# Branching to the experts' widths before the first expert is prepared, with its first weights requested in the stage before

## The chip, the cores and the metric

The kernel runs on one NeuronCore of one Trainium2 chip. The metric is the device time of one execution in microseconds (us), as the median of repeated runs.

## The reference, cut to what matters

The program is one macaron block on 8 x 1024 tokens of 512 float32 values: half an expert layer, a self-attention layer, half an expert layer again, with a layer norm ahead of each.

```python
x = x + 0.5 * ffn(layernorm(x), w_router, w_gate, w_up, w_down)
x = x + attention(layernorm(x), Wq, bq, Wk, bk, Wv, bv, Wo, bo)
x = x + 0.5 * ffn(layernorm(x), w_router, w_gate, w_up, w_down)

def ffn(x, ...):                      # T = 8192 tokens, E = 32 experts, C = 320 rows for each
    probs = softmax(xt @ w_router)
    top1 = argmax(probs); gate = probs[top1]
    pos = (number of earlier tokens with the same top1)
    accepted = pos < C
    buf[top1, pos] = xt               # accepted tokens, by expert
    y = (silu(buf @ w_gate) * (buf @ w_up)) @ w_down
    return xt + where(accepted, y * gate, 0)
```

Every expert has three weight matrices of 512 x 512 (1 MB each). Which token goes to which expert, and how many each expert gets, is known only at run time.

## The kernel before, in words

The program has five parts in a row: the routing of all tokens (`front`), the experts (`experts`, first call), the attention (which routes its own results as it goes), and the experts again (second call). PE, ScalarE (ACT), VectorE (DVE) and GpSimd (POOL) run their instructions in the order in which the code writes them ("by hand"); SyncE (SP) issues the plain DMAs, in their order too.

**Routing.** Tokens are worked on in tiles of 128. `front` forms groups of tiles (4, then seven times 8, then 4). For each group `route` finds each token's expert, its place and its slot, and then GpSimd scatters a pair (token, gate) for every token into a table in HBM, with one indirect DMA for each tile (line 331). The tile `row` that these DMAs read has two buffers, so the row of one group waits for the scatters of the group two before it (lines 304 and 305). In the last group `sorted` ranks the experts by their number of tokens: it leaves a permutation `matrix`, the experts' `order` (line 466) and `arm`, the number of the narrowest of three width profiles that covers the counts (line 471).

**Experts, preparation.** `experts` has a preparation (lines 510 to 535) that holds for all profiles, then a `Switch` on `arm` into one of three copies of the loop over 32 experts. The preparation issues, on SP: the three weights of the first expert (line 578, by way of `load`), then the read of the whole table as `slots` (line 513, 96 KB). The table is reordered by two matmuls (line 519) into the row numbers `come` (to gather), `go` (to scatter) and the `gates`. GpSimd then gathers the rows of the first two experts, three blocks of up to 128 tokens each (line 587). The first expert is measured (`measure`: statistics of three blocks, line 151, then one power on GpSimd for all three, line 163), normalized on ACT (line 172), scaled for the residual on DVE (`rests`, line 186), and transposed (`transpose`: for each of four column parts k, three PE transposes and one copy on DVE, lines 658 and 661).

**Experts, loop.** `feed` computes one expert and prepares the next: measure the next, gather the one after that, then for each of four parts f the products with `w_gate` and `w_up` (line 670, accumulators `gp` and `up` with two buffers each), the gating on ACT and DVE (lines 675 and 694), at last the product with `w_down` (line 709) and an indirect DMA that scatters the results (line 727). The first call also moves tokens without a place (`all`, lines 600 to 615). The weights of the first expert lie in the preparation's pool, the others in a pool with two buffers inside the branch.

**Order on SP.** The first weights of the first call wait for the whole of `front`, its last scatter too: their memory is that of the routing's tiles. The attention begins with DMAs of the biases, the rotary tables and its weights.

Of the kernel before, what the change touches and what calls it, by code (L numbers as in the profile page):

```python
# [13 lines left out]
F32 = mybir.dt.float32  # L14
I32 = mybir.dt.int32
BF16 = mybir.dt.bfloat16
AF = mybir.ActivationFunctionType
ALU = mybir.AluOpType
AX = mybir.AxisListType
PSUM = bass.MemoryType.PSUM  # L20
DRAM = bass.MemoryType.DRAM

P = 128
# [5 lines left out]
G = 8  # L29
# [6 lines left out]
def at_once(steps):  # L36

    while True:
        try:
            next(steps)  # L40
        except StopIteration as end:
            return end.value
# [8 lines left out]
class Block:  # L51
# [287 lines left out]
    def front(self, pool, psum, x, rest, spare, carry, table, ranked):  # L339
# [2 lines left out]


        nc, NT, D, KD, E = self.nc, self.NT, self.D, self.KD, self.E
        sizes = [G // 2] + [G] * (NT // G - 1) + [G // 2]
        starts = [sum(sizes[:i]) for i in range(len(sizes))]
        group = [g for g, size in enumerate(sizes) for _ in range(size)]
        mv = pool.tile([P, NT, 2], F32, name="mv", bufs=1)
# [53 lines left out]
        for i in range(-ahead, NT + 2):  # L402
# [19 lines left out]
            t = i + ahead  # L422
# [49 lines left out]

        return (matrix, order, arm), rest()

    def experts(self, table, ranks, src, dst, w_gate, w_up, w_down, others=None):

        nc, tc, E, T = self.nc, self.tc, self.E, self.T
        NB, n = self.NB, self.last
        views = dram_disjoint_views(dst, E * NB + (self.NT if others else 0))
        weights = [w.rearrange("e (k p) f -> e p k f", p=P) for w in (w_gate, w_up, w_down)]
        F = mybir.EngineType
        by_hand = {F.PE, F.Activation, F.DVE, F.Pool}
        with tc.tile_pool(name="et", bufs=1) as tp:
            R = NB * E  # L490
            matrix, order, arm = ranks
            come, go = tp.tile([P, R], I32, name="come"), tp.tile([P, R], I32, name="go")
            at = [tp.tile([P, R], F32, name=f"at{i}") for i in range(2)]
            ids, gates = at

            def load(expert, r):
                e = nc.values_load(
                    order[0:1, r : r + 1], engines=[F.SP], min_val=0, max_val=E - 1,
                    skip_runtime_bounds_check_because="the number of a column of E",
                )  # L500
                return expert.load([w[e] for w in weights])

            acts = self.acts
            with (
                tc.tile_pool(name="ef", bufs=1) as fp,
                tc.tile_pool(name="efps", bufs=2, space=PSUM) as ps,
                tc.manual_schedule(engines=by_hand),
            ):

                expert = Expert(self, (tp, tp, ps), src, views, come, go, gates, acts)  # L510
                first = load(expert, 0)
                rows = fp.tile([R, P, 2], F32, name="slots")
                nc.sync.dma_start(
                    rows, table[0 : self.NS, :].rearrange("(r s) c -> r s c", s=P)
                )
                nc.vector.tensor_copy(rows[R - E : R, n:P, :], rows[R - E : R, 0:n, :])
                for i in range(2):
                    pt = ps.tile([P, R], F32, tag="tp", name="pt")
                    nc.tensor.matmul(pt, rows[:, :, i], matrix, start=True, stop=True)
                    if i == 0:  # L520
                        nc.vector.tensor_scalar(come, pt, float(T - 1), None, ALU.min)
                    nc.vector.tensor_copy(at[i], pt)
                states = [expert.gather(r, self.C) for r in range(2)]
                nc.vector.tensor_copy(go[:, 0 : R - E], ids[:, 0 : R - E])
                for i in range(2):
                    nc.vector.tensor_scalar(
                        go[i * n : (i + 1) * n, R - E : R], ids[i * n : (i + 1) * n, R - E : R],
                        2.0, float(i), ALU.mult, ALU.add,
                    )
                states[0].weights = first  # L530
                expert.measure(states[0])
                expert.scales(states[0])
                expert.normalize(states[0])
                expert.rests(states[0])
                expert.transpose(states[0])
            which = nc.values_load(
                arm[0:1, 0:1], min_val=0, max_val=len(self.profiles) - 1,
                skip_runtime_bounds_check_because="a sum of so many comparisons",
            )
            for i in tc.Switch(which, len(self.profiles)):  # L540
                with (
                    tc.tile_pool(name="ew", bufs=2) as wp,
                    tc.tile_pool(name="ea", bufs=2) as ap,
                    tc.tile_pool(name="eps", bufs=2, space=PSUM) as ps,
                    tc.manual_schedule(engines=by_hand),
                ):
                    expert = Expert(
                        self, (wp, ap, ps), src, views, come, go, gates, acts, others
                    )
                    now, following = (SimpleNamespace(**vars(state)) for state in states)  # L550
                    for r in range(E):
                        if following:
                            following.weights = load(expert, r + 1)
                        after = None
                        if r + 2 < E:
                            after = lambda: expert.gather(r + 2, self.profiles[i][r + 2])
                        now, following = following, expert.feed(now, following, after)


class Expert:  # L560


    def __init__(self, s, pools, src, views, come, go, gates, acts, others=None):
        self.s, self.nc, self.others = s, s.nc, others
        self.wp, self.ap, self.ps = pools
        self.src, self.views = src, views
        self.come, self.go, self.gates, self.acts = come, go, gates, acts

        self.xs = 3 if self.wp is not self.ap else 2

    def load(self, weights):
        nc, s = self.nc, self.s
        tiles = [
            self.wp.tile([P, k, d], F32, tag=name, name=name)
            for name, k, d in (("wg", s.KD, s.F), ("wu", s.KD, s.F), ("wd", s.KF, s.D))
        ]
        for t, w in zip(tiles, weights):
            nc.sync.dma_start(t, w)
        return tiles

    def gather(self, r, width):

        nc, s = self.nc, self.s
        NB = -(-width // P)
        x = self.ap.tile([P, s.NB, s.D], F32, tag="x", bufs=self.xs, name="x")
        for i in range(NB):
            nc.gpsimd.indirect_dma_start(
                out=x[:, i, :], out_offset=None, in_=self.src,
                in_offset=bass.IndirectOffsetOnAxis(
                    ap=self.come[:, i * s.E + r : i * s.E + r + 1], axis=0  # L590
                ),
            )
        return SimpleNamespace(r=r, width=width, NB=NB, x=x)
# [84 lines left out]
    def feed(self, now, following, after):  # L678
# [2 lines left out]

        nc, s = self.nc, self.s
        n, half, KF = s.last, s.D // 2, s.KF
        a, wd = self.acts[now.r % 2], now.weights[2]
        others = self.fetch_others(now.r) if self.others else None
        if following:
            self.measure(following)
# [663 lines left out]
def tile_macaron(  # L1351
# [22 lines left out]

    rest = [const.tile([P, NT], F32, name=f"rest{i}") for i in range(2)]
    spare = const.tile([P, NT], I32, name="spare")
    ranking = ctx.enter_context(tc.tile_pool(name="ranking", bufs=1))

    xf = x.rearrange("b l d -> (b l) d")
    of = out.rearrange("b l d -> (b l) d")  # L1380


    F_ = mybir.EngineType
    with (
        tc.tile_pool(name="a", bufs=2) as pool,
        tc.tile_pool(name="aps", bufs=4, space=PSUM) as psum,
        tc.manual_schedule(engines={F_.PE, F_.Activation, F_.DVE, F_.Pool}),
    ):
        none = pool.tile([P, s.NS // P, 2], F32, tag="none", bufs=1, name="none")
        nc.gpsimd.memset(none[:, :, 0], float(T))  # L1390
        nc.gpsimd.memset(none[:, :, 1], 0.0)
        for table in tables:
            nc.scalar.dma_start(
                table[0 : s.NS, :].rearrange("(p r) c -> p r c", p=P), none
            )
        ranks = []

        def ranked(counts):
            found, steps = s.sorted(ranking, psum, "lp", counts)
            ranks.extend(found)  # L1400
            return steps

        s.front(pool, psum, xf, rest, spare, zero, dram_disjoint_views(tables[0], NT), ranked)

    s.experts(tables[0], ranks, xf, x1, w_gate, w_up, w_down, (*rest, spare))


    attention = Attention(
# [2 lines left out]
    )  # L1411
    attention.run()

    s.experts(tables[1], attention.ranks, x2, of, w_gate, w_up, w_down)


def rope(L):
# [38 lines left out]
```

## Time and profile before

| what | us |
|---|---|
| median of 3 runs | 4938.32 (4932.55 to 4940.38) |
| the profiled execution: its time | 4953.15 |
| the profiled execution: its span, first to last instruction | 4951.4 |
| PE busy in the span | 4649.6 (94%) |
| DVE, ACT, POOL busy | 2842.6, 2923.9, 789.8 |

The mean granted TensorE clock is 0.969 of full speed. Times in the profile are microseconds from the start of the span. A row of the timeline gives the start, the busy time, the engine, the line of the kernel and what is written from what; in brackets stands the idle time before it, and what ended that. "PEld" is PE's weight load, "SPq" and "POOLq" are an engine's instruction queue. A DMA row gives the time to issue it; when its data has landed is seen from who waited for it. The chain of waits follows what ended last back to what released it.

### The profile page before, as it was taken

To read this page: it belongs to the slowest core of one execution; us is meant where nothing else is said; L and a number is where in the kernel's file an instruction comes from. 1 tells how busy PE (TensorE), PEld (TensorE's weight loads), DVE (VectorE), ACT (ScalarE), POOL (GpSimd) and SP (SyncE) were. 2 spreads that over 40 slices of the span, in tenths; PEclk is the share of its full clock that TensorE was granted. 3 is DMA by queue.
4 is the path that set the end of the run, shared out by engine and by line. 5 is a ranking of instruction groups with operands and counts; after the bars stand their busy time and mean duration, and the time that the engine had idled before them with its cause. 6 is when DMAs were issued, how large, how long until landed. Compare 5 with 4: busy or idle time off the path is not lost.

```text
span 4951.4 us, 68819 instructions
## 1 busy us (share of the span) xinstructions
PE 4649.6 (94%) x24568; PEld 2134.3 (43%) x24568; DVE 2842.6 (57%) x5530; ACT 2923.9 (59%) x5851; POOL 789.8 (16%) x779
## 2 busy tenths in 40 slices
PE   6499999969899999999999999999999876999998
PEld 4266667733233333333333333333333224666676
DVE  8333333337666777777777767767777633333332
ACT  6111112118999888888888888888888821111111
POOL 4323333210000010110110110100001002222221
PEclk8699999979999999999999999999999988999999
DMA  4355556630111212212212212212212124445553
GB/s 139 118 170 180 186 188 203 216 90 25 39 33 48 76 41 63 71 42 67 69 41 65 69 42 66 70 42 62 64 44 59 46 66 152 160 163 165 170 183 134
DMA packets 290535, 486.04 MB, mean 98 GB/s; under 512 B 47847, under 2 KB 83121, under 8 KB 290176
## 3 DMA queue, kind: packets, MB, share of 16 engines
q1 hardware_dynamic: 255328, 404.36, 26.0%
q0 software_dynamic: 34560, 76.93, 5.1%
q8 instruction: 197, 3.23, 0.3%
q14 instruction: 162, 1.33, 0.1%
q10 hardware_dynamic: 288, 0.20, 0.0%
HBM read 380.11 MB, written 89.72 MB: 95 GB/s over the span
## 4 chain that ended last, share of the span: by engine, by line
PE 81%; DVE 8%; ACT 4%; issue 3%; DMA 2%; POOL 1%; SPq 1%; another core or an unknown queue 0%; DVEq 0%; POOLq 0%; ACTq 0%
PE sa L1184 13%; PE gp L670 10%; PE up L670 9%; PE pq L1089 9%; PE po L1266 9%; PE yp L709 8%; PE sb L1164 5%; PE px L1292 4%; PE pv L1134 4%; PE sb L1191 3%; ACT junk L1203 2%; DVE nm L1199 2%; PE tp L658 2%; PE tp L194 2%; PE yp L717 1%
## 5 line engine op out<-in xcount | busy, mean ns | idle before, releaser
L1199 DVE TENSOR_REDUCE nm<-sa 128x2 f32<-128x1024 f32 x1024 | 1249.7, 1221 | 653.5 <-PE sa L1184 390.1
L1203 ACT ACTIVATE junk<-sa,nm 128x512 f32<-128x512 f32 x2048 | 1408.6, 688 | 256.1 <-DVE nm L1199 176.9
L1184 PE MATMUL sa<-k,q 32*128 32x512 f32 x4096 | 1150.4, 645 | 17.9 <-ACT junk L1203 11.5
L1196 ACT ACTIVATE pr<-sb 128x1024 f32<-128x1024 f32 x1024 | 1041.5, 1019 | 100.8 <-PE sb L1191 96.2
L1191 PE MATMUL sb<-q,k 32*128 32x512 f32 x4096 | 1062.8, 602 | 0.0
L675 ACT ACTIVATE sg<-gp 128x320 f32<-128x320 f32 (+3 forms) x256 | 103.0, 402 | 1228.7 <-PE gp L670 1091.7
L1266 PE MATMUL po<-pr,v 128*32 128x512 f32 x4096 | 549.5, 608 | 0.1
L1114 POOL TENSOR_TENSOR raw<-raw,a 128x512 f32<-128x512 f32 x128 | 165.0, 1289 | 2400.8 <-DMA rot<-raw 1638.9
L670 PE MATMUL gp<-bT,wg 128*128 128x320 f32 (+3 forms) x2048 | 532.6, 403 | 7.0 <-DVE n L167 6.2
L670 PE MATMUL up<-bT,wu 128*128 128x320 f32 (+3 forms) x2048 | 525.0, 399 | 0.0
L1089 PE MATMUL pq<-hT,wqk 128*128 128x512 f32 x1024 | 511.2, 623 | 4.7 <-DVE raw L1104 3.6
L709 PE MATMUL yp<-wd,a 128*128 128x512 f32 x1024 | 453.7, 596 | 0.0
L670 PEld LDWEIGHTS gp<-bT,wg 128*128 128x128 f32 x2048 | 387.6, 191 | 122.9 <-issue 35.6
L1164 PE MATMUL sb<-mrow,ones 3*128 3x512 bf16 x2048 | 393.8, 385 | 41.7 <-ACT pr L1196 40.0
L694 DVE TENSOR_TENSOR a<-sg,up 128x320 f32<-128x320 f32 (+3 forms) x256 | 114.1, 446 | 554.1 <-PE up L670 515.0
L670 PEld LDWEIGHTS up<-bT,wu 128*128 128x128 f32 x2048 | 389.2, 190 | 94.4 <-issue 0.2
L1164 PEld LDWEIGHTS <-ones 3*128 3x128 bf16 x2048 | 99.9, 91 | 710.8 <-issue 668.8
L1203 ACT ACTIVATION_READ_ACCUMULATOR junk<-sa,nm 128x1 f32 x2048 | 398.3, 195 | 0.0
L1191 PEld LDWEIGHTS sb<-q,k 32*128 32x128 f32 x4096 | 360.2, 184 | 0.1
L1184 PEld LDWEIGHTS sa<-k,q 32*128 32x128 f32 x4096 | 305.5, 184 | 80.7 <-ACT pr L1196 29.3
L1089 PEld LDWEIGHTS pq<-hT,wqk 128*128 128x128 f32 x1024 | 176.1, 191 | 323.5 <-issue 227.7
L713 DVE SCALAR_TENSOR_TENSOR ys<-yp,at,x 128x512 f32<-128x512 f32 x128 | 96.1, 751 | 369.0 <-PE yp L709 369.0
(171 smaller groups left out, 4275.0 us busy)
## 6 DMA issues: line engine op xcount, KB each, us to landing
wg<-in_w_gate SPq DMA_DIRECT2D x64, 1024.0 KB
wu<-in_w_up SPq DMA_DIRECT2D x64, 1024.0 KB
wd<-in_w_down SPq DMA_DIRECT2D x64, 1024.0 KB
rot<-raw SPq DMA_DIRECT2D x1024, 32.0 KB
xq<-in_x SPq DMA_DIRECT2D x16, 1024.0 KB
all<-in_x SPq DMA_DIRECT2D x32, 512.0 KB
xt<-first_rows SPq DMA_DIRECT2D x64, 256.0 KB
xr<-first_rows SPq DMA_DIRECT2D x64, 256.0 KB
```

The lines of the kernel that those rows point to most:

```text
L670: nc.tensor.matmul(acc, w[:, k, f * P : (f + 1) * P], to.bT[:, k, 0:width], start=(k == 0), stop=(k == s.KD - 1),)
L709: nc.tensor.matmul(yp, a[:, f, i * P : (i + 1) * P], wd[:, f, :], start=(f == 0), stop=(f == KF - 1),)
L1089: nc.tensor.matmul(acc, w[:, which, k, :], self.hT[b, n][:, k, :], start=(k == 0), stop=(k == KD - 1),)
L1134: nc.tensor.matmul(acc, hT[:, k, at : at + P], self.w_vo[:, k, :], start=(k == 0), stop=(k == KD - 1),)
L1164: nc.tensor.matmul(sb[:, h, :], self.ones16[at : at + 3, :], row[at : at + 3, :], start=True, stop=False,)
L1184: nc.tensor.matmul(sa[:, h, :], qa[at, (g * 4 + j) * P : (g * 4 + j + 1) * P], ka[at, m * 512 : (m + 1) * 512], start=True, stop=True,)
L1191: nc.tensor.matmul(sb[:, h, :], k[at, t * P : (t + 1) * P], q[at, n * 512 : (n + 1) * 512], start=False, stop=True,)
L1196: nc.scalar.activation(pr, sb, AF.Exp)
L1199: nc.vector.tensor_reduce(nm[:, m, j, pair : pair + 2], sa, AX.X, ALU.max, negate=True)
L1203: nc.scalar.activation(self.junk, sa[:, h - pair, :], AF.Exp, bias=nm[:, m, j, h : h + 1], accum_out=se[:, m, j, h : h + 1],)
L1266: nc.tensor.matmul(self.po[at : at + HD, :], self.v[b][t][:, c * P + at : c * P + at + HD], prs[h // 2 * 2][:, h % 2, :], start=(t == 0), ...
L1292: nc.tensor.matmul(acc, self.oT[b, c, half][:, j * P : (j + 1) * P], self.w_vo[:, c, :], start=False, stop=(c == KD - 1),)
```

## The change

There are four edits.

1. `front` splits the last group of 8 tiles into two of 4 (`sizes`).
2. After the routing, in its by-hand section, SP is given the loads of the weights of the first two experts of the first call, into a pool `et` with two buffers that is opened ahead of the routing's pools and closed after the experts. The second call of `experts` gets no loaded weights.
3. The `Switch` moves to the beginning of `experts`. Everything that was the preparation is now written in each of the three branches. In a branch the table is read first (`places`), then the first expert is gathered with the width of that profile; in the second call the weights of the first expert are requested after that.
4. The first expert is prepared by `begin`, block by block: statistics, power, normalization and four PE transposes for one block of tokens after the other, into four PSUM tiles at once; then the four copies, two on DVE and two on ACT; the scaling for the residual (`rests`) comes last, and the gather of the second expert after it in the code.

```diff
-        sizes = [G // 2] + [G] * (NT // G - 1) + [G // 2]
+        sizes = [G // 2] + [G] * (NT // G - 2) + [G // 2] * 3
...
+    def load(self, pool, order, r, weights):
+        nc = self.nc
+        e = nc.values_load(
+            order[0:1, r : r + 1], engines=[mybir.EngineType.SP], min_val=0,
...
+        for name, w in zip(("wg", "wu", "wd"), weights):
+            t = pool.tile([P, w.shape[1] // P, w.shape[2]], F32, tag=name, name=name)
+            nc.sync.dma_start(t, w.rearrange("e (k p) f -> e p k f", p=P)[e])
...
+    def experts(self, table, ranks, src, dst, weights, loaded=(), others=None):
...
+        which = nc.values_load(
+            arm[0:1, 0:1], min_val=0, max_val=len(self.profiles) - 1,
...
+        for i in tc.Switch(which, len(self.profiles)):
+            widths = self.profiles[i]
...
+                expert = Expert(self, (wp, ap, ps), src, views, others)
+                expert.places(table, matrix)
+                def load(r):
+                    return loaded[r] if r < len(loaded) else self.load(wp, order, r, weights)
+                now = expert.gather(0, widths[0])
+                now.weights = load(0)
+                expert.begin(now)
+                following = expert.gather(1, widths[1])
+                for r in range(E):
+                    if following:
+                        following.weights = load(r + 1)
...
+    def begin(self, to):
...
+        for i in range(to.NB):
+            at = slice(i, i + 1)
+            s.stats(ap, to.mv[:, i, :], to.x[:, i, :])
+            steps.append(s.normalizing(ap, to.mv[:, at, :], [t[:, at] for t in to.by]))
+            next(steps[i])
+            if i:
+                at_once(steps[i - 1])
+        at_once(steps[-1])
...
+        for i in range(to.NB):
+            s.normalize(to.b[:, i, :], to.x[:, i, :], to.by, i)
+            m = min(P, C - i * P)
+            for k, tp in enumerate(tps):
+                nc.tensor.transpose(
+                    tp[:, i * P : i * P + m], to.b[:m, i, k * P : (k + 1) * P],
+                    s.ident[:m, :m],
+                )
+        for k, tp in enumerate(tps):
+            (nc.scalar.copy if k % 2 else nc.vector.tensor_copy)(to.bT[:, k, 0:C], tp[:, 0:C])
+        self.rests(to)
...
+    first = ExitStack()
+    et = first.enter_context(tc.tile_pool(name="et", bufs=2))
...
         s.front(pool, psum, xf, rest, spare, zero, dram_disjoint_views(tables[0], NT), ranked)
+        loaded = [s.load(et, ranks[1], r, weights) for r in range(2)]
+    s.experts(tables[0], ranks, xf, x1, weights, loaded, (*rest, spare))
+    first.close()
...
-    s.experts(tables[1], attention.ranks, x2, of, w_gate, w_up, w_down)
+    s.experts(tables[1], attention.ranks, x2, of, weights)
```

`places` holds the lines of the old preparation that read the table and form `come`, `go` and `gates`, unchanged but for the pool of their tiles.

## The prediction

> **What bounds the kernel now.** I read the page first: busy shares, then the chain. Expert loops and attention are limited by PE, which nothing here changes: PE is busy 99.8 of 100 us in the stretch 309 to 409. The edits lie in the two places where PE idles: routing to first expert product (first call: PE's last routing product ends about 154, first `gp` at 209.41) and attention's end to the same product (`gp` at 4129.61). As each expert loop runs at PE's pace, an earlier first `gp` moves all that follows. So I ask for each call what ends last before `gp`. The chain of waits of the second call (start, length):
>
> ```profile
> 4094.49 2.13 DMA table<-row,slot
> ...
> 4098.86 9.90 DMA slots<-table
> ...
> 4113.83 7.13 DMA x<-x,come
> ...
> 4128.86 0.50 DVE bT L661
> ...
> 4129.61 4.61 PE gp L670 x8
> ```
>
> The reader sees serial work: last scatter, a table read of 9.90 us for 96 KB, the gather of token rows, and, in lines left out here, statistics, normalization and PE's ten transposes (3.12 us) up to the copy. Then the timeline of the first call:
>
> ```profile
> 169.06 0.96 POOL L331 DMA_INDIRECT table<-row,slot  x1 [0.31 <-issue]
> 171.73 0.39 SPq L578 DMA_DIRECT2D wg<-in_w_gate  x1
> 172.33 0.38 SPq L578 DMA_DIRECT2D wu<-in_w_up  x1
> 172.90 0.37 SPq L578 DMA_DIRECT2D wd<-in_w_down  x1
> 173.32 0.63 SPq L513 DMA_DIRECT2D slots<-table  x1
> 183.25 0.22 DVE L516 COPY slots<-slots 32x128 f32<-32x128 f32 x1 [24.52 <-DMA slots<-table]
> ...
> 193.27 0.69 DVE L151 BATCH_NORM_STATS2 st<-x 128x6 f32<-128x512 f32 x1 [7.55 <-DMA x<-in_x,come]
> ...
> 203.22 0.49 DVE L661 COPY bT<-tp 128x320 f32<-128x320 f32 x1 [0.42 <-PE tp L658]
> ...
> 209.41 3.88 PE L670 MATMUL gp<-bT,wg 128*128 128x320 f32 x8 [6.22 <-DVE n L167]
> ```
>
> The table read stands behind three weights in SP's queue. The last copy ends at 203.71, yet `gp` starts at 209.41; in the second call the same step takes 0.26 us (4129.35 to 4129.61). `gp` doesn't read `n`, so the releaser named is chance. Between copy and `gp` PE has only the Switch. The DMA answer for 204 to 209:
>
> ```profile
> DMA  9999999999999999999999999999999999999999
> ...
> q8 instruction: 1, 0.02, 1.4%
> ```
>
> The DMA engines are at nine tenths or more throughout, nearly all of it SP's queue (1.89 MB), and one block of code (0.02 MB, queue q8) comes in. I read the 5.4 us (5.70 less 0.26) as PE's fetch of the branch's code through busy DMA engines.
>
> **First call: Switch moved (edit 3).** All engines need `arm` only, ready at 157.28; PE, ACT and DVE then have nothing to do until the table lands at 183.25, so their jumps and fetches lie under that wait. Gain: PE's 5.4 us. [...] If the cover is gone, every engine that still waits for code pays about 5.4.
>
> **First call: weights early, table behind them (edit 2).** The weights no longer wait for the last scatter but for `order`. That looks like a gain of 15 us (156.42 to 171.73), but the table read stays behind them, and it is now 6 MB. Before, from the issue of `wg` to the table landed took 11.52 us with 3 MB; the queue moved some 395 GB/s, so 3.15 MB more are 8.0, in all 19.5. Also SP's queue holds under 4 MB (the third `wd` took 8.32 us to issue at 189.75, with 5.5 MB ahead): SP is held about 9 us in the issues before it reaches its own jump; within the 19.5.
>
> `order` itself comes later by edit 1. In the built order of DVE the chains of the last three groups of 4 are interleaved. Adding rows of the trace from 138.03 on: the four operations of the next group (0.32 each) and its ranking (1.7) now stand before the slots of tiles 44 to 51, so their scatters start at 144.5, not 141.34. The `row` of tiles 56 to 59 must wait until those 8 scatters (1.265 each) have landed: 155.5. Then follow 1.7 us of ranking, 0.8 for PE's count, 1.4 of sorting, 1.6 of slots, 1.2 of row: `order` at about 163, the last scatter ends at 171.6 (before 170.02). SP's first weight issues at 163.7 and the table lands at 163.7 + 19.5 = 183.2, against 183.25: **nothing gained**. Ends: `order` as before at 157 gives 177, 6 us better; scatters that land late under the weights (7.5 us, as a gather takes, not 2.13) end by 178, under the queue, at no cost; 3 us worse if SP's jump itself costs a fetch that leaves the queue empty.
>
> **Second call: table first.** SP's jump lies before the last scatter landed (4096.62). The table issues at 4097.2, as `wg` did, nothing ahead. How long alone? The nearest rows: a scatter 2.13 from its issue, and the program's first `xq` (1 MB, empty queue) 5.66, less 2.7 of data at 395 GB/s: 3.0. [...] A plain read from HBM is nearer to `xq`: with 3.0 it lands at 4100.2; before, DVE took it at 4108.88 (0.05 of it sequencer). Gain 8.6; ends 9.5 (2.13) and 5.7 (if POOL's own jump, begun at 4095.5, costs a fetch under load, ready 2 to 3 us after the row numbers). First weights now follow the table: 3 MB in by about 4108, long before `gp`; free.
>
> The gather after the table keeps its price: 2.47 from table to first gather, 7.5 to its first block, since weights fill the queues in both calls as before.
>
> **Preparation by blocks (edit 4).** Before, first block landed to `gp`: 4118.87 to 4129.61, 10.74. Now, from that landing (0), with the same rows: statistics with aggregate and the add 1.1 for a block; blocks land 1.1 apart. Power with its handovers 1.18, so block 0 has its factors at 2.4 (DVE is busy with block 1), ACT normalizes it 2.6 to 3.4; block 1 at 4.1, block 2 at 5.1 to 5.85 (0.8 each), four transposes of 64 columns to 6.5. Copies, 0.49 each, two on DVE beside two on ACT: first pair at 7.05. `gp` at 7.3. Gain **3.4** in each call: three serial things shrink, PE's 3.1 us of ten transposes, four copies in turn, and the residual scaling (2.1 us), which now runs on DVE under the first products. Powers go from one of 0.89 to three; POOL does them under DVE. Behind them in POOL's queue is the gather of the second expert: issued at 4.7 after landing, in by about 14 under load; DVE waits there for it with the first `a` behind it. PE has two `up` buffers and stalls only if `a` isn't done by 7.3 + 12.4 = 19.7; forecast 16.9. Free, with 2.8 us to spare.
>
> The `SiLU` table load (1.28 us, ACT) goes ahead of `gp`; ACT isn't late: 0. [...] its eight products may take the 4.61 of the second call, not 3.88: cost 0.7.
>
> **Attention's start.** In the built order of SP the three bias loads (issued 1024.11 to 1025.38) no longer wait for the last scatter of the experts, and `bo`, `wvo`, `xt` move up: gain 1.4, between 0 (if they queue elsewhere) and 1.5.
>
> **Sum.** First call 5.4 + 3.4 + 0.0 - 0.7 = 8.1. Second 8.6 + 3.4 = 12.0. Attention 1.4. Together 21.5 us: from the profiled span of 4951.4 to 4929.9. That execution took 4953.15, 14.8 above the median; the difference is taken from the median: 4938.3 - 21.5 = **4916.8**.
>
> **Rivals.**
>
> *The first call gains as well at the table* (chance 0.15): DVE's order costs less than I add up, `order` comes at 157. Then 6 us more: 4911. For: my sum adds rows that may overlap. Against: the wait of `row` for 8 scatters is in the program.
>
> *The first call gains nothing* (0.21): 6 MB ahead of the table, a late `order`, a late second gather (each us past 19.7 counts) or a PE jump that wasn't code take its 8.1: 4925, to 4929. For: the queue is shown full. Against: 5.4 us between copy and `gp` have no other owner.
>
> *It doesn't reach the end* (0.08): what is won is lost again where the loops or attention start: 4935. Against: PE is 99.8% busy there.
>
> *Slower: the jumps now lie on the path* (0.05). Place: after the Switch each engine of the chain table, `come`, gather, statistics, normalize, transpose starts on cold code while 6 MB of weights fill the DMA engines; fetches that come after an engine's data cost 5.4 each. With four exposed in all (of ten, five engines in two calls) the gain of 21.5 is gone; with seven: 7 x 5.4 = 38 less 21.5, so 4955. For: the PE stall at 203.71. Against: in the first call engines have 10 to 20 us between jump and data; in the second POOL has 7.
>
> *As summed*: 0.51, with 4911 to 4922 for the small terms.
>
> **Chances and range.** About 0.2%, 9.9 us, can be told from no change. Faster than 4928.4: as summed, the first rival, and nearly all of the second: 0.85. Same: the third and the second's edge: 0.10. Slower: 0.05. The range 4904 to 4929 takes in the first two rivals.
>
> **What would show it.** First call: PE, DVE, ACT and POOL jump before the table lands; no gap between the last copy and `gp`; table at about 183, in spite of weights issued at 164; `gp` near 201. Second call: table read issued before `wg`, landed 3 us later, `gp` near 4117 on the old clock, 12 us less from the last scatter to `gp`. In both, 7.3 us from first block to `gp`. It would be wrong if engines show idle time of "issue" for some 5 us inside the branches before the first `gp`, or if `order` is ready well before 163.

## The result, and the profile after

The changed kernel takes 4914.68 us (median of 5; 4911.93 to 4919.01), the kernel before on the same chip 4934.31 (median of 5): a ratio of 0.9958, with a 95% interval of 0.9943 to 0.9972, so 19.6 us less. The forecast was 4916.8, which is 21.5 less than the 4938.32 on record then (median of 3). On a second chip, where both kernels took longer, the ratio was 0.9951 (0.9937 to 0.9964; 4929.19 against 4954.69, 25.5 us less). As the absolute times differ by chip, everything below is compared by its ratio to the kernel before on the same chip, or by distances inside one trace.

The profiled execution of the changed kernel took 4919.01 us, with a span of 4917.2; PE is busy 4646.1 of it (94%), as before. Where the time went is read from the two stages in which PE idles. The timeline of the changed kernel in the first call (start, busy time, engine, line; in brackets the idle time before it):

```profile
147.50 0.39 SPq L485 DMA_DIRECT2D wg<-in_w_gate  x1
...
153.79 3.51 SPq L485 DMA_DIRECT2D wd<-in_w_down  x1
154.57 0.97 POOL L331 DMA_INDIRECT table<-row,slot  x1 [0.30 <-issue]
162.65 0.35 SPq L553 DMA_DIRECT2D slots<-table  x1
...
171.54 0.22 DVE L554 COPY slots<-slots 32x128 f32<-32x128 f32 x1 [22.29 <-DMA slots<-table]
...
180.33 0.69 DVE L151 BATCH_NORM_STATS2 st<-x 128x6 f32<-128x512 f32 x1 [6.19 <-DMA x<-in_x,come]
...
187.18 4.63 PE L692 MATMUL gp<-bT,wg 128*128 128x320 f32 x8 [0.26 <-DVE bT L600]
```

The weights are requested at 147.50, before the last scatter (154.57), and yet the table is taken only at 171.54. Between the end of the last scatter on GpSimd (155.54) and the issue of the table read stand 7.1 us, in which SyncE waits until the last scatter has landed (its semaphores come in from 158.5 to 162.6); then 8.9 us until the table is taken. PE's idle time in front of `gp` is 0.26 us, where it was 6.22. The stretches of the same trace between these events (start:end, length, busy time and count of PE, PEld, DVE, ACT, POOL, granted clock, DMA share, GB/s):

```profile
147.50:155.50 8.00, 0.00 (x0) 0.00 (x0) 1.55 (x10) 0.00 (x0) 6.16 (x7) 0.50 0.86 259
155.50:162.60 7.10, 0.00 (x0) 0.00 (x0) 0.00 (x0) 0.00 (x0) 0.04 (x1) 0.50 1.01 284
162.60:171.50 8.90, 0.00 (x0) 0.00 (x0) 0.00 (x0) 0.00 (x0) 0.00 (x0) 0.50 1.05 377
```

For 16 us no compute engine has anything to do: the core waits for weights that nobody needs yet, because a table of 96 KB is behind them. In the first two stretches, with scatters under way, the DMA engines moved 259 and 284 GB/s, in the third, without them, 377. Part of the first figure is the start of the first transfer (the engines' busy share is 0.86 there); in the second the engines are fully busy and still move a quarter less. The second call, in which the table goes first:

```profile
4077.49 0.34 SPq L553 DMA_DIRECT2D slots<-table  x1
4078.37 0.41 SPq L485 DMA_DIRECT2D wg<-in_w_gate  x1
...
4079.53 0.22 DVE L554 COPY slots<-slots 32x128 f32<-32x128 f32 x1 [9.17 <-DMA slots<-table]
...
4082.05 0.98 POOL L609 DMA_INDIRECT x<-x,come  x1 [6.58 <-DVE go L564]
...
4088.08 0.69 DVE L151 BATCH_NORM_STATS2 st<-x 128x6 f32<-128x512 f32 x1 [5.96 <-DMA x<-x,come]
...
4094.90 1.43 PE L692 MATMUL gp<-bT,wg 128*128 128x320 f32 x2 [0.26 <-DVE bT L600]
```

The same read takes 2.04 us here. It is 15.4 us from the table to `gp`, against 20.7 in the kernel before (4108.88 to 4129.61).

All profiles on one sheet. "Scatter to gp" runs from the end of the last scatter on GpSimd to the first product; "table" from the issue of its read until VectorE takes it; "block to gp" from the first gathered block measured. All in us, first call / second call. These distances don't contain the routing, and are the better measure of the edits: most of the versions' intervals overlap, so that their times alone can't rank them.

| kernel | ratio to before, 95% | scatter to gp | table | block to gp |
|---|---|---|---|---|
| before, profile shown above | 1 | 39.4 / 34.2 | 9.9 / 10.0 | 16.1 / 10.7 |
| before_again | timed once | 39.7 / 34.6 | 10.2 / 10.2 | 16.2 / 10.8 |
| changed kernel | 0.9958 (0.9943 to 0.9972) | 31.6 / 19.4 | 8.9 / 2.0 | 6.9 / 6.8 |
| after_again | 0.9951 (0.9937 to 0.9964) | 31.5 / 20.3 | 10.2 / 2.0 | 6.9 / 7.2 |
| switch_fixed | 1.0003 (0.9994 to 1.0011) | 36.6 / 36.2 | 10.0 / 9.8 | 13.2 / 12.7 |
| old_prep | 0.9968 (0.9957 to 0.9980) | 34.8 / 23.4 | 8.7 / 2.0 | 10.7 / 10.1 |
| table_line | 0.9956 (0.9943 to 0.9970) | 29.2 / 24.0 | 2.0 / 2.0 | 16.7 / 11.3 |
| no_split | 0.9946 (0.9932 to 0.9959) | 27.5 / 20.0 | 6.0 / 2.0 | 6.9 / 6.4 |
| table_act | 0.9949 (0.9936 to 0.9963) | 28.3 / 20.0 | 6.0 / 2.1 | 6.9 / 6.5 |
| one_early | 0.9934 (0.9921 to 0.9948) | 23.2 / 19.9 | 2.2 / 2.1 | 6.7 / 6.4 |
| table_first | 0.9927 (0.9913 to 0.9940) | 20.3 / 19.5 | 2.1 / 2.1 | 6.9 / 6.9 |
| quiet_gather | 0.9923 (0.9909 to 0.9936) | 17.8 / 17.0 | 2.0 / 2.1 | 6.4 / 6.9 |
| quiet_no_split | 0.9921 (0.9907 to 0.9934) | 17.9 / 17.0 | 2.1 / 2.0 | 6.4 / 7.0 |

### The profile page after: what moved, and what is told of

Its sections match the earlier page's. It is cut to its first block, busy times and chain, and to the rows that moved or that the text cites. A ratio compares the mean times of both kernels' runs of the same rounds, so it can differ in the third digit from the quotient of the medians.

```text
span 4917.2 us, 68877 instructions
## 1 busy us (share of the span) xinstructions
PE 4646.1 (94%) x24572; PEld 2133.2 (43%) x24572; DVE 2847.5 (58%) x5568; ACT 2925.1 (59%) x5856; POOL 789.9 (16%) x784
## 4 chain that ended last, share of the span: by engine, by line
PE 81%; DVE 8%; ACT 4%; issue 3%; DMA 2%; POOL 1%; SPq 1%; DVEq 0%; POOLq 0%; ACTq 0%
PE sa L1206 13%; PE gp L692 10%; PE up L692 9%; PE pq L1111 9%; PE po L1288 9%; PE yp L731 9%; PE sb L1186 5%; PE pv L1156 4%; PE px L1314 4%; PE sb L1213 3%; ACT junk L1225 2%; DVE nm L1221 2%; PE tp L680 2%; PE tp L194 1%; PE yp L739 1%
## 5 line engine op out<-in xcount | busy, mean ns | idle before, releaser
L1206 PE MATMUL sa<-k,q 32*128 32x512 f32 x4096 | 1150.0, 645 | 19.4 <-ACT junk L1225 12.0
L735 DVE SCALAR_TENSOR_TENSOR ys<-yp,gates,x 128x512 f32<-128x512 f32 x128 | 96.1, 751 | 369.0 <-PE yp L731 369.0
```

Source lines behind the costliest of these rows:

```text
L1206: nc.tensor.matmul(sa[:, h, :], qa[at, (g * 4 + j) * P : (g * 4 + j + 1) * P], ka[at, m * 512 : (m + 1) * 512], start=True, stop=True,)
```

## The experiments

**Theory:** in both calls the table read is what ends last; the gain comes from what shortens the way through it, and in the first call the early weights take back part of it. **Rivals:** the weights had to come early, the Switch is the main part, or the difference is of the routing (the profiled execution before was 34 us longer than the one after, of which 19.6 are the medians').

**before_again** and **after_again**: both kernels unchanged, for second profiles.

> The kernel before, unchanged, for a second profile. Theory: the idle time of 13.43 us of GpSimd ahead of the scatter at 141.34 belongs to that one execution (it took 14.8 us more than the median), so it is not here: last scatter at about 156.6, table at 169.9, first gp at about 196, span about 4937. The idle time of 5.4 us of PE between the last copy and gp is of the program and is here again. Rival 1: the idle time ahead of the scatter is here again, gp at 209. Rival 2: the 5.4 us are not here, and were part of the same disturbance.

> The changed kernel, unchanged, for a second profile and a second measurement. In four of the six profiles so far ScalarE stood idle for 13.4 to 13.7 us in all in the routing (before copies at 115 to 131, with nothing in the trace that released it), in one 7.2, in the profiled execution of the changed kernel not at all. Theory: this idle time is of the execution, not of the change, so it can be here too, and the last scatter is then issued at about 169 to 170; from the last scatter's end to the first gp it takes 31.6 us as in the first profile, against 39.4 in both profiles of the kernel before. Rival: it is of the change (another order of the routing's work avoids it), and the last scatter is at about 155 again.

The first expectation fell (its rival 1, that the idle time is there again, holds), and the second came true. The kernel before, again; what ScalarE waited for between 110 and 135 (us in total, times, longest):

```profile
ACT lg L240 <- remote: 6.5, 1, 6.5
ACT xT L408 <- remote: 5.3, 1, 5.3
ACT parts L230 <- remote: 1.6, 1, 1.6
```

The changed kernel, again; its timeline of ScalarE:

```profile
114.04 0.59 ACT L408 COPY xT<-tp 128x512 f32<-128x512 f32 x1
120.72 0.27 ACT L240 COPY lg<-lp 128x128 f32<-128x128 f32 x1 [6.10 <-remote]
120.89 0.81 ACT L172 ACTIVATE h<-xq,nmr,rstd 128x512 f32<-128x512 f32 x1
125.00 0.58 ACT L408 COPY xT<-tp 128x512 f32<-128x512 f32 x1 [3.29 <-remote]
129.99 0.58 ACT L230 COPY parts<-pl 128x512 f32<-128x512 f32 x1 [4.41 <-remote]
```

ScalarE stands idle for 13.4 and 13.8 us at the same three copies, with no releaser in the trace, in both kernels. Such idle time of 12.2 to 13.8 us in all (in table_first 7.2) is in the first profile of the kernel before (whose 4953.15 us are a time of the slower chips) and in all eight of the two chips on which that kernel takes 4951 and 4955 us. It is not in the first profile of the changed kernel, nor in the four of the chip on which the kernel before takes 4935. So in these 14 profiles it goes with the chip and not with the change, and comparing the first two profiles span by span would have credited the change with some 14 us that are not its own. The distances behind the routing repeat: 39.4 and 39.7 before, 31.6 and 31.5 after.

**table_first**: the early weights taken away.

```
-        loaded = [s.load(et, ranks[1], r, weights) for r in range(2)]
-    s.experts(tables[0], ranks, xf, x1, weights, loaded, (*rest, spare))
+    s.experts(tables[0], ranks, xf, x1, weights, (), (*rest, spare))
```

> The changed kernel, but the first call requests its weights as the second does: inside the branch, behind the table read; nothing is requested in the routing's section. Theory (the early weights hold up the table): in the changed kernel the last scatter landed some 7 us after its issue and the table was taken at 171.54, 8.9 us after the issue of its read. Without the 6 MB ahead the last scatter (issued 155.5) lands in about 2, the table 2.04 after that as in the second call: taken at about 159.7. From there the second call needs 15.4 to its first gp (4079.53 to 4094.90): gp at about 175 instead of 187.18, the time about 12 us less than the changed kernel, 4902 to 4904. Rival (early weights are needed at gp): the 3 MB, requested only at about 162, share the queues with the gather and the second expert's 3 MB, and gp waits for them: gp between 184 and 190, time 4912 to 4918.

Its timeline in the first call:

```profile
167.12 0.97 POOL L331 DMA_INDIRECT table<-row,slot  x1 [0.30 <-issue]
169.81 0.35 SPq L553 DMA_DIRECT2D slots<-table  x1
170.70 0.41 SPq L485 DMA_DIRECT2D wg<-in_w_gate  x1
...
171.89 0.22 DVE L554 COPY slots<-slots 32x128 f32<-32x128 f32 x1 [10.08 <-DMA slots<-table]
...
188.36 4.63 PE L692 MATMUL gp<-bT,wg 128*128 128x320 f32 x8 [0.27 <-DVE bT L600]
```

From the last scatter's end (168.09) to the table's issue 1.7 us, to the table 2.1, to `gp` 20.3 in all: 11.3 less than in the changed kernel, where 12 were expected. PE's idle time in front of `gp` is 0.27, so no weight is late. The whole takes 37.5 us less than the kernel before, against 19.6 and 25.5 for the changed kernel. (Its 4913.94 lies among the times that were expected of the rival, but these were formed on the first chip; on this one the kernel before takes 4951.39.) The early weights cost about a third of what the rest of the change gains: by the ratios 0.0024 to 0.0031 of 0.0073, by the distances 11.3 of 33.8 us.

**one_early** and **table_act**: only 3 MB early (`range(1)`, one buffer); and all 6 MB early with the table read on ScalarE's queue.

```
-        nc.sync.dma_start(rows, table[0 : s.NS, :].rearrange("(r s) c -> r s c", s=P))
+        (nc.scalar if self.others else nc.sync).dma_start(rows, table[0 : s.NS, :].rearrange("(r s) c -> r s c", s=P))
```

> The changed kernel, but only the first expert's weights (3 MB, not 6) are requested in the routing's section. Theory: these 3 MB, issued from 147.5, are in by about 158.5, when the last scatter (issued 155.5) can land by 159 to 160; the table follows by 162 and gp by 177 to 178: some 9 us less than the changed kernel, 4905 to 4907. Rival (it is not the bytes ahead that hold up the table): table at 171 as before, time within 2 us of the changed kernel's 4914.7.

> The changed kernel with the 6 MB early, but in the first call the table read is issued on ScalarE's queue instead of SyncE's. If the table is held up by its place in SyncE's queue, it now lands 2 to 5 us after its issue at about 162.7 (between 165 and 168, instead of 171.54), and the time falls by 4 to 7 us, to 4908 to 4911; the late landing of the last scatter (7 us) remains. If the DMA engines themselves serve the bytes in the order in which they were requested, whatever the queue, it lands at 171 again and the time is 4914 to 4916.

The last scatter, the issue of the table read and the copy that takes it; first one_early, then table_act (ACTq is ScalarE's queue):

```profile
170.49 0.97 POOL L331 DMA_INDIRECT table<-row,slot  x1 [0.30 <-issue]
...
176.25 0.36 SPq L553 DMA_DIRECT2D slots<-table  x1
...
178.42 0.22 DVE L554 COPY slots<-slots 32x128 f32<-32x128 f32 x1 [13.25 <-DMA slots<-table]
```

```profile
170.25 0.97 POOL L331 DMA_INDIRECT table<-row,slot  x1 [0.30 <-issue]
...
177.89 0.40 ACTq L553 DMA_DIRECT2D slots<-table  x1
...
183.84 0.22 DVE L554 COPY slots<-slots 32x128 f32<-32x128 f32 x1 [18.90 <-DMA slots<-table]
```

With 3 MB the last scatter still lands late (4.8 us from its end to the table's issue), but the table then has nothing ahead of it and takes 2.2: scatter to `gp` 23.2, 8.4 less than the changed kernel (9 expected). On its own queue the table takes 6.0 us, neither 2 nor the 8.9 and 10.2 of the changed kernel: some of the delay is the place in SyncE's queue, and some goes with the weights still under way (some 2.3 MB at its issue, an estimate: 6.3 MB less what the DMA engines would have moved in 14.7 us at the changed kernel's 259 and 284 GB/s). The last scatter, on a queue of its own too, landed 6.7 us after its end, where it was 7.1 and 5.6 in the changed kernel. Scatter to `gp` is only 3.3 shorter, and the ratio moves by 0.0002 to 0.0009, within the intervals; 4 to 7 us were expected. The hold-up has to be removed at the bytes, not only at the queue.

**table_line**: the kernel before with one line moved, `first = load(expert, 0)` behind the table's `dma_start`.

> The kernel before with one line moved: the read of the table is issued ahead of the first expert's weights, in both calls. Theory (the table's place in SyncE's queue is the largest part of the change): it is taken 2 us after its issue instead of 9.9 to 10.2 in both calls, so gp comes 8 to 9 us earlier in each, 16 to 18 us less than the kernel before. Rival (the weights or the gather take the place of the table): the 3 MB of weights are then late for the gather or for gp, and no more than 8 us are gained in all.

Its timeline in the first call:

```profile
171.73 0.35 SPq L512 DMA_DIRECT2D slots<-table  x1
...
173.76 0.22 DVE L516 COPY slots<-slots 32x128 f32<-32x128 f32 x1 [14.92 <-DMA slots<-table]
...
193.17 0.49 DVE L661 COPY bT<-tp 128x320 f32<-128x320 f32 x1 [0.42 <-PE tp L658]
...
199.29 3.88 PE L670 MATMUL gp<-bT,wg 128*128 128x320 f32 x8 [6.16 <-DVE n L167]
```

Scatter to `gp` falls by 10.2 in each call, more than forecast, because the gather comes in after 6.4 us instead of 7.5 as well. In time 22.8 us less, where the whole change gives 25.5 on the same chip; the intervals overlap. PE's gap in front of `gp` (193.66, the last copy's end, to 199.29) is still there, so it has nothing to do with the table.

**switch_alone** and **switch_fixed**: the kernel before with only the Switch moved ahead of the preparation. Of the edit, as switch_fixed has it, the lines that matter:

```
-        with tc.tile_pool(name="et", bufs=1) as tp:
+        for arm_i in tc.Switch(which, len(self.profiles)):
+            with tc.tile_pool(name="et", bufs=1) as tp:
...
-                            after = lambda: expert.gather(r + 2, self.profiles[i][r + 2])
+                            after = lambda: expert.gather(r + 2, self.profiles[arm_i][r + 2])
```

> The kernel before with one edit only: the Switch ahead of the preparation, which is otherwise as before (first weights first, then the table; statistics, normalization and transposes in the old order). Theory (PE's idle time ahead of the first gp is the fetch of the branch's code): 0.3 us between the last copy and gp instead of 5.7, so from the last scatter's end to gp 34 us instead of 39.4; no change in the second call, where the gap was 0.26. About 5 us less than the kernel before. [...] Rival 2 (the fetch comes at another place): engines show idle time of some 5 us inside the branch before gp, and the time is as before or slower.

> The Switch moved alone, as in the run switch_alone, with its fault mended: there an inner loop wrote over the number of the profile, so that every branch took the middle profile's wider products and both loops of experts were longer (some 30 us each). What that run showed up to the first gp stands: 0.58 us between the last copy and gp instead of 5.7, code blocks fetched at 155 to 162 instead of at 205, and 35.7 us from the last scatter's end to gp instead of 39.4; in the second call 35.7 instead of 34.2. Expected with the loops as before: first call 3 to 4 us less, second 1 to 2 us more, in all 1 to 3 us less than the kernel before. Rival (the second call's loss was of the fault too): 4 to 5 us less.

The first of them (ratio 1.0120, 1.0104 to 1.0135) had an inner loop that wrote over the number of the profile, so that all branches computed with the middle profile's widths; its loops are some 30 us longer each, and it says something only up to the first `gp`. The second is as meant, and gains nothing (1.0003), where 1 to 3 us were expected. Its timeline in the first call:

```profile
183.04 0.69 DVE L151 BATCH_NORM_STATS2 st<-x 128x6 f32<-128x512 f32 x1 [0.56 <-DMA x<-in_x,come]
...
187.72 1.90 PE L659 MATMUL tp<-ident,b 128*128 128x128 f32 x6 [1.67 <-DVE bT L662]
...
189.66 0.49 DVE L662 COPY bT<-tp 128x320 f32<-128x320 f32 x1 [0.42 <-PE tp L659]
190.21 0.50 PEld L671 LDWEIGHTS gp<-bT,wg 128*128 128x128 f32 x2 [0.77 <-DVE bT L662]
190.21 1.43 PE L671 MATMUL gp<-bT,wg 128*128 128x320 f32 x2 [0.58 <-DVE bT L662]
```

PE's idle time in front of `gp`, 6.22 us in the kernel before, is 0.58 here (from the last copy's end, 190.15, it is 0.06 instead of 5.70): that step is right. But once preparation and loop stand in one branch, their order on VectorE mixes: the statistics of the second expert's blocks (the one at 183.04 is the third of them) go ahead of the first expert's copies, and PE's transposes wait for those (1.67). Block to `gp` is 13.2 and 12.7 rather than the 10.7 expected without a gap: from scatter to `gp` 2.8 are gained in the first call and 2.0 lost in the second. In the changed kernel the second gather, and so its statistics, stand behind `begin`, and this doesn't occur.

**old_prep**: the changed kernel without `begin`; in its place `measure`, `scales`, `normalize`, `rests`, `transpose`.

> The changed kernel with edit 4 undone: inside the branch the first expert is prepared in the old order (all statistics, one power, all normalizations, residual scaling, then for each column part its transposes and one copy on VectorE), nothing else changed. Theory: from the first block to gp about 10.7 us instead of 6.85 in both calls, 7 to 8 us more than the changed kernel in all. Rival (the copies and transposes hide behind the arrival of the weights or the fetch of code): under 3 us more.

Its first call, from the first block to the last copy:

```profile
178.48 0.69 DVE L151 BATCH_NORM_STATS2 st<-x 128x6 f32<-128x512 f32 x1 [6.27 <-DMA x<-in_x,come]
...
189.15 4.63 PE L696 MATMUL gp<-bT,wg 128*128 128x320 f32 x8
189.26 0.49 DVE L687 COPY bT<-tp 128x320 f32<-128x320 f32 x1 [0.42 <-PE tp L684]
```

Block to `gp` is 10.7 and 10.1 us instead of 6.9 and 6.8 to 7.2: `begin` is worth 3.7 to 3.8 and 2.9 to 3.3. The ratio of 0.9968 is 0.0010 to 0.0017 above the changed kernel's, 5 to 8 us; its interval overlaps the changed kernel's two. Its 10.7 in the first call, against 16.1 in the kernel before with the same order of work, is also the cleanest measure of the Switch: 5.5 us. The lines show something that the prediction didn't have: with preparation and loop in one branch, `gp` starts before the last of the four copies does (189.15 against 189.26). In the second call, where the kernel before has no long gap, the moved Switch still brings 10.1 instead of 10.7.

**no_split**, **quiet_gather**, **quiet_no_split**: the last groups of tiles 8 and 4 as before; the version of table_first with all weights but the first `wg` held back; and both together. The holding back is a write of one element that the DMA has to follow, on VectorE after the statistics of the first block (for the first expert's `wu` and `wd`) or of the last (for the second expert's weights):

```
+        for j in which:
+            if hold:
+                nc.vector.memset(tiles[j][0:1, 0, 0:1], 0.0)
```

> The changed kernel with edit 1 undone: the last groups of tiles 8 and 4 as before. Theory (the split makes order late and so the early weights): order is ready about 5 us earlier (156.5 against 161.0 where ScalarE stood idle for some 13.5 us), the 6 MB start earlier and most of them are through when the last scatter is in; the table is taken at 178 to 180 instead of 185.7 in the second profile of the changed kernel, and the time is 5 to 7 us less than the changed kernel's. Rival (the last scatter is what counts, and the split brings it no later or even earlier): within 2 us of the changed kernel.

> The version with the table first in both calls and no early weights, and with the other weights held back: only the first expert's wg (1 MB) is requested behind the table; its wu and wd are requested when the first gathered block has been measured, the second expert's weights when the last block has been. (A one-element memset on VectorE holds each DMA back.) Theory (the gather's 6.0 to 7.0 us from issue to first block are time behind 3 to 6 MB of weights): the first block lands 3 to 4 us after its issue, gp comes 3 us earlier in each call, and the time is about 6 us less than with the table first alone. Rival 1 (the gather takes that long by itself): no difference at the block, the same time. Rival 2 (wu is now late): PE waits for wu after the first four products of gp, and the gain is lost again.

> The version with the table first in both calls and the other weights held back (quiet_gather), with edit 1 undone as well. Nothing is requested in the routing here, so only the last scatter's time counts. With the split and with about 13.5 us of idle ScalarE it was issued at 168.9 to 170.5, without the split at 168.1 to 169.3. Expected: gp 0 to 1.5 us earlier, the same time as quiet_gather within 2 us. Rival (the split does bring the last scatter earlier, as the two profiles of other idle times would allow): 1 to 2 us slower.

Without the split `order` is ready at 139.31 where it was 146.79 in the changed kernel's first profile (both without the idle time of ScalarE before these copies), the table takes 6.0 us, with some 5.1 of the 6.3 MB through at its issue (an estimate, again at 259 and 284 GB/s), and scatter to `gp` is 4.1 shorter; the ratio moves by 0.0005 to 0.0012, 2 to 6 us, within the intervals. With nothing requested early no difference of the split can be told (0.9921 and 0.9923). What it costs shows only in the distance, by way of the early weights.

Holding back the weights shortens the gather. In quiet_gather, second call:

```profile
4081.91 0.98 POOL L638 DMA_INDIRECT x<-x,come  x1 [6.66 <-DVE go L592]
...
4085.33 0.70 DVE L151 BATCH_NORM_STATS2 st<-x 128x6 f32<-128x512 f32 x1 [3.35 <-DMA x<-x,come]
```

The first block is there 3.4 us after its gather, instead of 6.1 in table_first; in the first call 5.1 instead of 7.0, as SyncE put the read of the tokens without a place (1 MB) ahead of it. Scatter to `gp` is 2.5 shorter in each call. That 5 us show in the time is not settled: the ratio is 0.0004 (2 us) below table_first's, within the intervals, where 6 us were expected. quiet_no_split has the lowest ratio of all, 0.9921 (0.9907 to 0.9934), 4895.37 against 4935.01 of the kernel before: 39.6 us less. By the ratios that is 1.6 to 1.9 times the change's gain.

## Why the prediction was right, step by step

The way of the change and most of its terms came out as forecast. That the sum came within 2 us is in part luck: from the last scatter to `gp` the first call gained 7.8 to 8.1, where the terms make 10.4 (5.4 + 3.4 and, with the last scatter 1.6 later and the table as before, 1.6), and the second 14.3 to 14.7, where they make 12.0. On a clock like that of the profile from which the forecast was made (after_again, with the same idle time of ScalarE) `order` came at 161.0 (forecast 163), the table at 185.68 (183.2) and `gp` at 201.45 (near 201). By the distances of the sheet:

- **Switch moved, 5.4:** right, and shown twice (old_prep's 10.7 against 16.1; in switch_fixed 0.06 us from the last copy to `gp` instead of 5.70). That it is a fetch of code fits: in the gap of the kernel before, a block of code (0.02 MB, queue q8) comes in between 206.4 and 207.0, and in that of table_line between 196 and 198 (before_again has one somewhere between 160 and 210); in the second call of the kernel before, without the gap, it comes at 4132, behind the start of the first `gp`; and in switch_alone it came in between 155 and 160, ahead of the table, and none from 160 to 205. But the trace doesn't say for which engine a block is, so the cause is inferred from this timing, and why the second call could do without the block stays open. That a moved Switch alone would keep the 5.4 was not claimed and isn't so.
- **Table behind 6 MB, "nothing gained":** the mechanism was right, a size wrong. The term "the queue moved some 395 GB/s, in all 19.5" measured 24.0 (147.50 to 171.54): until the last scatter had landed the DMA engines moved 259 and 284 GB/s, and the table read, issued only then, still had some 2.2 MB of weights ahead of it (an estimate: 6.3 MB less what these rates make in 15.1 us). Against the end of the last scatter the table came at 16.0 us, before at 13.2: a loss of 2.8, where the sum had a gain of 1.6 (11.6 us, 171.6 to 183.2). "At no cost" for the scatters that land late was wrong too: with nothing requested early the table is issued 1.7 us after the last scatter's end instead of 7.1, and from there to `gp` it is 11.3 us less (table_first).
- **`order` later by the split:** forecast 6.7 us later (163 against 156.33; the terms listed from 155.5 on add up to 162.2). The wait of `row` for the scatters is there: 4.75 us of idle VectorE up to 140.00 in the changed kernel's first profile. Versions with and without the split on chips of the same kind differ by 4.4 to 7.5. Last scatter: forecast 1.6 later, measured between 0.4 earlier and 2.6 later.
- **Table first in the second call, 8.6:** read 3.0 forecast, 2.04 measured. The value chosen, from `xq`, was too high; the lower bound (2.13, a scatter) was nearer. From the last scatter's end to the table it is 4.0 to 4.1 now and was 13.4 to 13.9: a gain of 9.4 to 9.9.
- **The gather keeps its 7.5:** wrong, in the changed kernel's two profiles it takes 6.0 to 6.6: 1.0 to 1.6 more gained in each call. quiet_gather shows that the number depends on what is queued ahead (5.1 in its first call, 3.4 in its second).
- **`begin`, 3.4 in each call:** forecast 7.3 from block to `gp`, measured 6.8 to 7.2. Against old_prep 3.7 to 3.8 and 2.9 to 3.3; in the second call some 0.7 more comes with the moved Switch, as `gp` starts before the last copy.
- **Clock, -0.7:** an estimate from the two calls of the profile before, where the first eight products took 3.88 (at a granted clock of 0.61) and 4.61 (at 0.50). In the first call of the changed kernel they took 4.63 (at 0.50) in one profile and 3.76 in the other: it varies without the change, and what sets it was not shown.
- **Second gather's margin:** in both calls of the first profile PE is busy 34.94 of the 35 us from the first `gp` on, at a granted clock of 0.93 and 0.92; in after_again it has no idle time in the 35 us of the first call, nor in the first 24 of the second: right.
- **Attention's start, 1.4:** the loads behind the biases are issued 2.99 us after the last result scatter, 4.40 before, as forecast. The first product with `wqk` then comes 42.8 us after the end of that scatter instead of 43.5 (in the second profiles 43.0 instead of 43.7): 0.7 to 0.8 is left. From the first `gp` of the first call to the last scatter of the attention it is 3888.3 and 3884.6 in the changed kernel's two profiles, 3886.0 and 3884.4 before: nothing that can be told.

In sum the two calls gain 22.1 to 22.8 between last scatter and `gp` (22.4 by the terms), less up to 2.6 where the split brings the last scatter later (forecast 1.6): between 19.5 and 23, beside the 19.6 and 25.5 of the medians (the interval of the second is 17.8 to 31.2). The rival in which exposed code fetches make it slower did not happen: in both profiles no engine has an idle time of over 1.1 us on "issue" inside the branch before `gp` but PE's weight load, whose 12.4 and 27.6 us lie under the wait for the table. The rival "the first call gains at the table" was nearest to what could have been had, but the lever was to request the weights later, not to have `order` earlier.

## What to carry to other kernels

A small transfer on which everything waits has to go ahead of the big ones that only need to be there later, and "ahead" means fewer bytes under way in the DMA engines, not only its place in a queue: prefetching 6 MB in idle time cost 11 us here, and on a queue of its own the table still took 6.0 us instead of 2.0. Moving one line gave 22.8 of the whole change's 25.5 us, so try the smallest reordering alone before a larger one. Before two profiles are compared span by span, take each a second time, and measure between events behind the stage that differs.

## What the runs showed of the hardware that was not expected

- ScalarE stood idle for 12.2 to 13.8 us (once 7.2) in the routing in all profiles on two chips, and in none on a third; the kernel before takes 16 to 20 us longer on the two. The DMA engines are nearly empty at the time (2 GB/s in before_again and 1 in after_again from 114 to 131, at a busy share of 0.02). The cause stays open.
- While the last scatters (8 bytes for each token) landed among the weights, the DMA engines, fully busy, moved less: 284 GB/s and then 377 in the changed kernel's first profile. That the scatters are the cause is likely but not shown, as no run has these weights without scatters. From the end of the last scatter on GpSimd to the next request on SyncE or ScalarE, which waits for its landing, it took 1.6 to 2.0 us with no weights requested early and 4.8 to 7.1 among the weights.
- A gather of 128 rows took 3.4 us from issue to data with 1 MB requested shortly ahead of it (quiet_gather, second call), 5.1 with 2 (its first call), and 6.0 to 7.6 with 3 MB or more (all versions that hold nothing back).
